# A four-layer network on one core: order of the scan directions, a stream of parts beside the scans, and six product buffers

## The chip, the core and the metric

The kernel runs on one core of a Trainium2 chip, and the metric is the time on the device in microseconds (us). A core has a matrix engine (PE, with its weight loads shown apart as PEld), a vector engine (DVE), a scalar engine for activation functions (ACT), a general engine (POOL) and an engine that issues transfers (SP). Each runs its own queue of instructions in order; they meet at semaphores. The kernel's time before the change is 23055.54 us, the median of three runs that lie between 23043.62 and 23061.29.

## The reference, cut to what matters

Eight images of 56 x 56 tokens with 192 channels go through four layers, each `x = x + layer(group_norm(x))`:

- layer 0 is a gated Toeplitz convolution along h and along w: `p * (o1 + o2) @ o_w`, with `p = silu(x @ p_w)`
- layer 1 is attention in shifted windows of 7 x 7 tokens
- layer 2 is a depthwise 3 x 3 convolution
- layer 3 is a selective scan in four directions:

```
xz = x @ in_proj_w.T; xi, z = split(xz); z = silu(z)
xc = silu(conv3x3(xi))
xs = stack([x_f, x_t, x_f reversed, x_t reversed])
h[t] = exp(delta[t] * A) * h[t-1] + delta[t] * u[t] * B[t]
y[t] = sum over n of h[n, t] * C[n, t] + D * u[t]
y = layer_norm(sum of the four directions) * z;  out = y @ out_proj_w.T
```

Here `x_f` runs through the tokens row by row and `x_t` column by column. There are 384 inner channels (three blocks of 128, index d) and 16 states (eight pairs, index k).

## The kernel before, in words

**Ahead of the scans.** The kernel first computes q * v of layer 0 and the Toeplitz products for all images and writes them to memory. Then it runs the front of image 0 alone. A front is a Python generator that joins five parts: `gate` (the rest of layer 0), `attention`, `conv2`, `inner` (the input projection, the convolution and the activations of layer 3) and `steps`. `steps` computes, in 14 pieces of 448 tokens, the step sizes delta and the coefficients B and C for the two directions of each token order o (o = 0 row by row, o = 1 column by column), and stores them to memory; each piece has one softplus (L870). In `inner` the convolution of a piece of 448 tokens is 9 matmuls into one bank (L802), which ACT then reads (L811). All parts of a front share one buffer, `slab`, so that they follow one another.

**The scans.** Image by image, four directions (slots 0 to 3: slots 0 and 1 row by row, forwards and backwards; slots 2 and 3 column by column), seven chunks of 448 tokens, three d and eight k: 5376 pairs, here also called steps of the loop. One pair g takes these operations:

- POOL: `inject` (L991), hs = du * B for two states
- ACT: two `decay` activations (L1006) into a PSUM bank, and two small copies for the state at the chunk's edge (L996, L1028)
- DVE: the scan itself (L1015)
- `times_c` (L1021), the product hc = h * C, on POOL for k = 1, 4 and 6, on DVE for the other five
- PE: `add_up` (L1036), which adds the two halves of hc into the bank ps_y by a matmul with the identity; the profile has four records for it

There are four hc buffers, so the product of pair g waits until `add_up` of pair g - 4 is done. After eight pairs `sums` adds ps_y into `ysum` (L1046 for slot 0, with the D * x term; L1050 for the other slots; in slots 2 and 3 the target is read and written in steps of a row). du = delta * x (L979, POOL) is made ahead for the next chunk from three loads of x (`load_xc`, L969).

**The parts beside the scans.** While the pairs of image b run, the front of image b + 1 is worked in. A planner, `Parts`, keeps a modelled time for each engine, and after each pair `parts.step` resumes the waiting generators as far as their next piece fits a limit for each engine: for PE up to 5 us after the modelled start of the next scan (n1 + 5.0). The instructions then stand in the engines' queues in the order in which they were emitted. The other kind of part is `finish(b, j)`: the layer norm, gating and output projection for one chunk of 448 tokens (L891 to L934), which reads `ysum`. Since slots 2 and 3 write every row of `ysum`, an image can be finished only after its last slot; its seven finishes therefore run beside slot 0 of the next image, each ahead of the sums that overwrite its tokens. Those of the last image run at the end by themselves.

Before the last chunk of an image's slot 3 ends (d = 1, k = 0 of that chunk, pair 656 of 672) the loads for the next image are issued. At that point a loop with the limit `anything` forces out whatever is left of the front of image b + 1.

Of the kernel before, what the change touches and what calls it, by code (L numbers as in the profile page):

```python
# [15 lines left out]
F32 = mybir.dt.float32  # L16
# [6 lines left out]
H = W = 56  # L23
# [58 lines left out]
def model(ctx: ExitStack, tc: tile.TileContext, a: dict, out: bass.AP):  # L82
# [197 lines left out]
    with (  # L280
# [79 lines left out]


        meter, costs = Meter(tc.nc), {}


        st = wp.tile([CP, 2, NCH, 6], F32, name="gn_st")
# [466 lines left out]
        def steps(b):  # L832

            w_x, xc, rc, dl = carve(slab, 128, (2, ND, 128), (2, ND, CH), (2, CH), (2, ND, CH))
            nc.sync.dma_start(out=w_x, in_=a["w_x"])
            todo = [(o, j) for o in range(2) for j in range(NCH)]

            def load_x(n):
                o, j = todo[n]
                nc.sync.dma_start(out=xc[:, n % 2], in_=xc_d[o][b][:, :, j * CH : (j + 1) * CH])  # L840

            load_x(0)
            yield 0, 0, 8.0
            for n, (o, j) in enumerate(todo):
                tok = slice(j * CH, (j + 1) * CH)
                if n + 1 < len(todo):
                    load_x(n + 1)
                yield 0, 1
                p = bank()
                for d in range(ND):  # L850
                    nc.tensor.matmul(p[:, :CH], w_x[:, o, d, :], xc[:, n % 2, d, :], start=d == 0, stop=d == ND - 1)
                yield 1, 0
                nc.scalar.copy(rc[:, n % 2, :], p[:, :CH])  # L853
                nc.sync.dma_start(out=bc_d[o][b][:, tok], in_=rc[64:, n % 2, :])
                for d in range(ND):
                    yield 0, 2
                    held = []
                    for s in range(2):
                        row = slice(32 * s, 32 * s + R)
                        held.append(bank())  # L860
                        nc.tensor.matmul(  # L861
                            held[s][:, :CH], w_dt[row, o, d * 128 : (d + 1) * 128], rc[row, n % 2, :], start=True, stop=True
                        )
                    yield 2, 0
                    for s in range(2):
                        nc.scalar.activation(
                            dl[:, s, d, :], held[s][:, :CH], AF.Identity, bias=dt_b[:, 2 * o + s, d : d + 1]
                        )
                yield 0, 0
                nc.scalar.activation(dl, dl, AF.Softplus)  # L870
                usual_functions()
                for s in range(2):
                    nc.sync.dma_start(out=dl_d[2 * o + s][b][:, :, tok], in_=dl[:, s])
            yield 0, 0

        def front(b):
# [61 lines left out]
        def scan_view(t, slot, j):  # L938

            if slot < 2:  # L940
                return t[:, j * CH : (j + 1) * CH].rearrange("p (u v) -> p u v", v=H)
            return t.rearrange("p (h w) -> p w h", w=W)[:, 8 * j : 8 * j + 8, :]
# [1 line left out]
        chunks = [  # L944
            (b, slot, j)
            for b in range(B)
            for slot in range(4)
            for j in (range(NCH - 1, -1, -1) if slot % 2 else range(NCH))
        ]
        pairs = [(i, d, k) for i in range(len(chunks)) for d in range(ND) for k in range(NP)]  # L950
# [14 lines left out]

        def load_xc(i, d):
            b, slot, j = chunks[i]
            t = sp.tile([128, CH], F32, name="xcd", bufs=4)
            nc.sync.dma_start(out=t, in_=xc_d[slot // 2][b][:, d, j * CH : (j + 1) * CH])  # L969
            return t  # L970

# [3 lines left out]
            nc.sync.dma_start(out=delta[:, :, 1 : CH + 1], in_=dl_d[slot][b][:, :, j * CH : (j + 1) * CH])  # L975

        def times_x(i, d):
            du = dus[i, d] = sp.tile([128, 1, CH], F32, name="du", bufs=4)
            nc.gpsimd.tensor_mul(du[:, 0, :], deltas[i][:, d, 1 : CH + 1], xcs.pop((i, d)))  # L979

        def tokens(i):
# [35 lines left out]
        def times_c(g):  # L1017
            i, d, k = pairs[g]
            h = hss[g] if on_pool(d, k) else das[g]
            hc = hcs[g] = sp.tile([128, NG, CH], F32, name="hc", bufs=4)  # L1020
            (nc.gpsimd if on_pool(d, k) else nc.vector).tensor_mul(hc, h[:, :, tokens(i)[0]], cms[i, k])  # L1021

        def keep_state(g):
# [15 lines left out]

        def sums(i, d):  # L1040
            b, slot, j = chunks[i]
            y = yps[i, d][:, :CH]
            tok = slice(j * CH, (j + 1) * CH)
            if slot == 0:
                x = xds.pop((i, d))
                nc.vector.scalar_tensor_tensor(ysum[:, d, tok], x, Dsum[:, d : d + 1], y, ALU.mult, ALU.add)  # L1046
                run("D", 0.68)
            else:
                yv = scan_view(ysum[:, d], slot, j)
                nc.vector.tensor_add(yv, yv, y.rearrange("p (u v) -> p u v", v=H))  # L1050
                run("D", 0.87)

        class Parts:

# [7 lines left out]
            def run(self, engine, cost, *after):  # L1062
                self.t[engine] = max(self.t[engine], 0.0, *after) + cost
                return self.t[engine]
# [25 lines left out]
                entry.held, entry.needs, *load = got  # L1090
                entry.ready = at + sum(load)

            def step(self, limit):
                old = [e for e in self.clients if e.held]
                for entry in old + [e for e in self.clients if e not in old]:
                    while entry in self.clients:
                        if entry.held and entry not in old:
                            break
                        if entry.needs + sum(e.held for e in self.clients if e is not entry) > 2:
                            break  # L1100
                        if not self.fits(entry, limit):
                            entry.waits += 1
                            break
                        entry.waits = 0
                        if entry in old:
                            old.remove(entry)
                        self.resume(entry)
# [16 lines left out]
        def drain(work, log=None):  # L1124

            while (next(work, None) if log is None else log_of(work, log)) is not None:
                pass
# [7 lines left out]
        with tc.manual_schedule():  # L1135
            for k in range(NP):
                load_bc(0, k)
            load_delta(0)
            for d in range(ND):
                xcs[0, d] = load_xc(0, d)  # L1140
                times_x(0, d)
            ahead, last = 2, len(pairs) - 1
            parts = Parts()
            run = parts.run
# [6 lines left out]

            def take(g):
                times_c(g)
                after = scanned[g], summed[g - 4] if g > 3 else 0.0
                taken[g] = run("P", 2.0, *after) if on_pool(*pairs[g][1:]) else run("D", 1.09, *after)

            def prepare(g):
# [4 lines left out]
                feed(g)  # L1162
            initial(0), initial(1)
            prepare(0)
            fronts = {}
            ending, anything = None, dict.fromkeys("ADE", 1e9)
            for g, (i, d, k) in enumerate(pairs):
                b, slot, j = chunks[i]
                if i % (4 * NCH) == 0 and d == 0 and k == 0 and b + 1 < B:
                    fronts[b + 1] = parts.add(front(b + 1), "front")  # L1170
                more = i + 1 < len(chunks)
                if more and d == 1 and k == 0:
                    if i + 1 in range(4 * NCH, len(chunks), 4 * NCH):
                        while fronts[b + 1] in parts.clients:
                            parts.step(anything)
                    load_delta(i + 1)
                    for e in range(ND):
                        xcs[i + 1, e] = load_xc(i + 1, e)
                if more and (d, k) in ((1, 6), (1, 7), (2, 0)):
                    times_x(i + 1, d + k - 7 if d == 1 else 2)  # L1180
                    run("P", 1.08)
                pi, pd, pk = pairs[g - 1]
                if g + ahead <= last:
                    feed(g + ahead)
# [14 lines left out]
                if g and pd == ND - 1 and pi + 1 < len(chunks):  # L1199
                    load_bc(pi + 1, pk)  # L1200
                done = (i, d - 1) if d else (i - 1, ND - 1)
                if k == 2 and g > NP and chunks[done[0]][1] == 0:
                    xds[done] = load_xc(*done)
                if slot == 0 and b > 0 and (d, k) == (1, 4):
                    while ending.at < 3:
                        parts.step(anything)
                if k == 4 and g > NP:
                    sums(*done)
                if slot == 0 and b > 0 and ((j, d, k) == (0, 0, 5) or j + 1 < NCH and (d, k) == (2, 4)):
                    while ending in parts.clients:  # L1210
                        parts.step(anything)
                    ending = parts.add(finish(b - 1, j + (d == 2)), "finish")

                n1 = max(parts.t["D"], fed[g + 1], set_[g + 1])
                n2 = n1 + (2.02 if on_pool(*pairs[min(g + 1, last)][1:]) else 3.11)
                parts.step({"A": max(n2, fed[g + 2]) - 0.7, "E": n1 + 5.0, "D": 0.2})
                if g >= 2:
                    add_up(g - 2)
                    summed[g - 2] = run("E", 1.1, taken[g - 2])
# [1 line left out]
                times_c(last)  # L1221
            for g in (last - 1, last):
                add_up(g)
            sums(i, d)
            for j in range(NCH):
                drain(finish(B - 1, j))


def constants():
# [98 lines left out]
```

## Time and profile before

| part of the span | us |
|---|---|
| start to the first scan (Toeplitz, front of image 0) | 3727 |
| image 0, first scan to first scan of image 1 | 2331 |
| images 1 to 6, each | 2453 to 2486 |
| image 7 | 2015 |
| last add-up to the end | 204 |

Busy shares of the span are PE 80%, DVE 72%, POOL 70%, ACT 54%, weight loads 42%. They average over the stages above, and the first stage has hardly any work for POOL. The columns of the views shown later are: for stages, the window, its length, the busy time of PE, PEld, DVE, ACT and POOL with the number of instructions, the share of full clock that PE was granted, the share of the transfer engines and GB/s; for waits, who waited for what, us in total, number of times, and the longest; for a timeline, start, duration, engine, line, operation, shapes and count, and in brackets the idle time ahead of it with what ended it.

### The profile page before, as it was taken

To read this page: it belongs to the slowest core of one execution; us is meant where nothing else is said; L and a number is where in the kernel's file an instruction comes from. 1 tells how busy PE (TensorE), PEld (TensorE's weight loads), DVE (VectorE), ACT (ScalarE), POOL (GpSimd) and SP (SyncE) were. 2 spreads that over 40 slices of the span, in tenths; PEclk is the share of its full clock that TensorE was granted. 3 is DMA by queue.
4 is the path that set the end of the run, shared out by engine and by line. 5 is a ranking of instruction groups with operands and counts; after the bars stand their busy time and mean duration, and the time that the engine had idled before them with its cause. 6 is when DMAs were issued, how large, how long until landed. Compare 5 with 4: busy or idle time off the path is not lost. (4 is left out here: it accounts for less than half of the span.)

```text
span 23083.3 us, 201064 instructions
## 1 busy us (share of the span) xinstructions
PE 18554.5 (80%) x58660; PEld 9730.9 (42%) x58660; DVE 16579.4 (72%) x13156; ACT 12534.0 (54%) x31864; POOL 16157.3 (70%) x8500
## 2 busy tenths in 40 slices
PE   8866678888887878888888888887888798887666
PEld 4566334434443435343543444343434353333323
DVE  3211114997789768986899778976898689877996
ACT  3211225655666565756565566656664657565554
POOL 0000004987789768976898778877897689778997
PEclk9987778999899989998999889998999899988888
DMA  3488225445544455345544454345534553454332
GB/s 89 109 196 178 67 62 171 135 123 168 167 135 131 142 169 146 124 135 172 151 134 129 161 162 137 122 147 177 148 115 146 168 157 119 140 172 139 126 122 89
DMA packets 2536339, 3220.44 MB, mean 140 GB/s; under 512 B 1045261, under 2 KB 2488687, under 8 KB 2504272
## 3 DMA queue, kind: packets, MB, share of 16 engines
q1 hardware_dynamic: 2515010, 3091.32, 45.2%
q0 software_dynamic: 15520, 116.14, 1.3%
q8 instruction: 465, 7.62, 0.1%
q14 instruction: 640, 5.24, 0.1%
q10 hardware_dynamic: 4704, 0.12, 0.0%
HBM read 2631.56 MB, written 575.48 MB: 139 GB/s over the span
## 5 line engine op out<-in xcount | busy, mean ns | idle before, releaser
L991 POOL TENSOR_TENSOR hs<-du,bm 128x896 f32<-128x896 f32 x5376 | 11124.4, 2102 | 110.1 <-DVE ps_a L1015 90.2
L1036 PE MATMUL ps_y<-hc,ident_sb 128*128 128x448 f32 x21504 | 9913.8, 597 | 947.8 <-POOL hc L1021 846.4
L1015 DVE TENSOR_TENSOR_SCAN ps_a<-ps_a,hs 128x898 f32<-128x898 f32 x3360 | 6793.9, 2022 | 1048.5 <-ACT ps_a L1006 871.5
L1006 ACT ACTIVATE ps_a<-delta,A_logs_sb 128x449 f32<-128x449 f32 x10752 | 6859.4, 638 | 322.2 <-DVE hs L1015 35.9
L1036 PEld LDWEIGHTS ps_y<-hc,ident_sb 128*128 128x128 f32 x21504 | 4339.0, 210 | 5095.4 <-issue 3594.3
L1021 POOL TENSOR_TENSOR hc<-hs,cm 128x896 f32<-128x896 f32 x2016 | 4067.0, 2017 | 2757.2 <-DVE hs L1015 1574.0
L1015 DVE TENSOR_TENSOR_SCAN hs<-ps_a,hs 128x898 f32<-128x898 f32 x2016 | 4064.5, 2016 | 810.3 <-ACT ps_a L1006 779.3
L1021 DVE TENSOR_TENSOR hc<-ps_a,cm 128x896 f32<-128x896 f32 x3360 | 3668.9, 1092 | 1166.1 <-PE ps_y L1036 883.2
L1028 ACT COPY state<-ps_a 128x2 f32<-128x2 f32 x3359 | 528.6, 157 | 4109.0 <-DVE hc L1021 4106.4
L979 POOL TENSOR_TENSOR du<-delta,xcd 128x448 f32<-128x448 f32 x672 | 716.0, 1066 | 1266.1 <-DMA xcd<-xc 1266.1
L263 PE MATMUL ps_tz<-tzx,tm 112*112 112x112 f32 x4608 | 889.3, 369 | 463.5 <-issue 294.7
L802 PE MATMUL ps_f<-slab 128*128 128x448 f32 x2646 | 1096.9, 551 | 85.0 <-DMA slab<-dg_d 58.0
L277 POOL DMA_DIRECT2D o<-tzx x192 | 97.8, 513 | 1490.9 <-DVE tzx L269 1340.1
L263 PEld LDWEIGHTS ps_tz<-tzx,tm 112*112 112x112 f32 x4608 | 883.8, 199 | 469.2 <-issue 468.1
L269 DVE COPY tzx<-ps_tz 112x448 f32<-112x448 f32 x288 | 179.9, 625 | 1172.3 <-PE ps_tz L263 862.0
L996 ACT COPY hs<-state 128x2 f32<-128x2 f32 x4608 | 817.5, 177 | 2.7 <-POOL hc L1021 2.6
L76 PE MATMUL ps_f<-slab 96*96 96x448 f32 (+6 forms) x2306 | 745.3, 519 | 76.1 <-DMA slab<-x 37.4
L269 ACT COPY tzx<-ps_tz 112x448 f32<-112x448 f32 x288 | 153.2, 532 | 1198.1 <-PE ps_tz L263 1067.2
L632 PE MATMUL ps_f<-ident_sb,slab 98*98 98x98 f32 x1344 | 337.9, 322 | 576.3 <-ACT slab L625 576.3
L734 PE MATMUL ps_f<-slab 96*96 96x448 f32 x1764 | 728.9, 549 | 46.4 <-DVE slab L721 46.4
L802 PEld LDWEIGHTS ps_f<-slab 128*128 128x128 f32 x2646 | 509.4, 193 | 598.0 <-issue 528.7
L861 PE MATMUL ps_f<-slab,w_dt_sb 12*128 12x448 f32 x1176 | 507.5, 787 | 309.8 <-ACT slab L853 234.9
(215 smaller groups left out, 17788.8 us busy)
## 6 DMA issues: line engine op xcount, KB each, us to landing
bm<-bc SPq DMA_DIRECT2D x1792, 448.0 KB
cm<-bc SPq DMA_DIRECT2D x1792, 448.0 KB
xcd<-xc SPq DMA_DIRECT2D x840, 224.0 KB
dl<-slab SPq DMA_DIRECT2D x224, 672.0 KB
delta<-dl SPq DMA_DIRECT2D x224, 672.0 KB
tzx<-qv SPq DMA_DIRECT2D x192, 588.0 KB
o<-tzx POOLq DMA_DIRECT2D x192, 588.0 KB, 16.3
slab<-x SPq DMA_DIRECT2D x224, 336.0 KB
```

The source lines that it names most:

```text
L76: return f(*args, **kw)
L263: nc.tensor.matmul(po[:, c, :], t[:, c2 + c, :], x[:, :, c1 + c2 + c], start=True, stop=True)
L734: nc.tensor.matmul(p[:CP, :CH], dg[:, k, t, :], xp[:, u, k, dy : dy + 8, dx : dx + W], start=t == 0, stop=t == 8,)
L802: nc.tensor.matmul(p[:, :CH], dg[:, t, :], xp[:, 8 * j + dy : 8 * j + dy + 8, dx : dx + W], start=t == 0, stop=t == 8,)
L979: nc.gpsimd.tensor_mul(du[:, 0, :], deltas[i][:, d, 1 : CH + 1], xcs.pop((i, d)))
L991: nc.gpsimd.tensor_mul(hs[:, :, tokens(i)[0]], dus[i, d].to_broadcast([128, NG, CH]), bms[i, k])
L996: nc.scalar.copy(hss[g][:, :, tokens(i)[1]], src)
L1006: nc.scalar.activation(dA[:, n, :], deltas[i][:, d, at : at + CH + 1], AF.Exp, scale=negA[:, slot, d, c : c + 1])
L1015: nc.vector.tensor_tensor_scan(h, dA, hs, 0.0, ALU.mult, ALU.add)
L1021: (nc.gpsimd if on_pool(d, k) else nc.vector).tensor_mul(hc, h[:, :, tokens(i)[0]], cms[i, k])
L1028: nc.scalar.copy(states[i][:, d, NG * k : NG * k + NG], h[:, :, tokens(i)[2]])
L1036: nc.tensor.matmul(yps[i, d][:, :CH], ident, hcs[g][:, n, :], start=k + n == 0, stop=k + n == NP + NG - 2)
```

## The change

Five things are altered together.

- The directions of an image go 2, 3, 0, 1: column by column first, row by row last, and the last one backwards. When a chunk of slot 1 is done, its tokens have all four directions, so its finish can start beside the following pairs of the same image. Only the last chunk's finish falls beside the next image, or for image 7 at the end. `steps` computes o = 1 first to match.
- The fronts form one stream. The front of the next image is added as soon as the one ahead is through, whichever image is being scanned. Instead of forcing out the whole front at the end of an image, the loop asks for each chunk whether its step sizes are there (`made`), and if not forces that front alone (`only`) up to that piece.
- There are six hc buffers in place of four.
- To make room for them, x and du have two buffers each in place of four, and are made one d at a time: the load at k = 0, the product at k = 3, for the d after the current one.
- The planner's limit for PE is n1 + 8.0 in place of n1 + 5.0.

The diff, cut to its core:

```diff
-            todo = [(o, j) for o in range(2) for j in range(NCH)]
+            todo = [(o, j) for o in (1, 0) for j in range(NCH)]
...
+                made.add((b, o, j))
...
-            for slot in range(4)
+            for slot in (2, 3, 0, 1)
...
-            t = sp.tile([128, CH], F32, name="xcd", bufs=4)
+            t = sp.tile([128, CH], F32, name="xcd", bufs=2)
...
-            du = dus[i, d] = sp.tile([128, 1, CH], F32, name="du", bufs=4)
+            du = dus[i, d] = sp.tile([128, 1, CH], F32, name="du", bufs=2)
...
-            hc = hcs[g] = sp.tile([128, NG, CH], F32, name="hc", bufs=4)
+            hc = hcs[g] = sp.tile([128, NG, CH], F32, name="hc", bufs=6)
...
-            if slot == 0:
-                x = xds.pop((i, d))
-                nc.vector.scalar_tensor_tensor(ysum[:, d, tok], x, Dsum[:, d : d + 1], y, ALU.mult, ALU.add)
+            if slot == 2:
+                x = xds.pop((i, d)).rearrange("p (u v) -> p u v", v=H)
+                nc.vector.scalar_tensor_tensor(yv, x, Dsum[:, d : d + 1], y, ALU.mult, ALU.add)
...
-                after = scanned[g], summed[g - 4] if g > 3 else 0.0
+                after = scanned[g], summed[g - 6] if g > 5 else 0.0
...
-                if i % (4 * NCH) == 0 and d == 0 and k == 0 and b + 1 < B:
-                    fronts[b + 1] = parts.add(front(b + 1), "front")
+                if ahead_of not in parts.clients and b_next < B:
+                    ahead_of = parts.add(front(b_next), "front")
+                    b_next += 1
...
-                    if i + 1 in range(4 * NCH, len(chunks), 4 * NCH):
-                        while fronts[b + 1] in parts.clients:
-                            parts.step(anything)
+                    b1, slot1, j1 = chunks[i + 1]
+                    while (b1, slot1 // 2, j1) not in made:
+                        parts.step(anything, ahead_of)
                     load_delta(i + 1)
-                    for e in range(ND):
-                        xcs[i + 1, e] = load_xc(i + 1, e)
-                if more and (d, k) in ((1, 6), (1, 7), (2, 0)):
-                    times_x(i + 1, d + k - 7 if d == 1 else 2)
-                    run("P", 1.08)
+                if k in (0, 3) and (d + 1 < ND or more):
+                    at = (i, d + 1) if d + 1 < ND else (i + 1, 0)
+                    if k == 0:
+                        xcs[at] = load_xc(*at)
+                    else:
+                        times_x(*at)
+                        run("P", 1.08)
...
-                if slot == 0 and b > 0 and ((j, d, k) == (0, 0, 5) or j + 1 < NCH and (d, k) == (2, 4)):
+                pb, pslot, pj = chunks[i - 1]
+                if i and pslot == 1 and (d, k) == (0, 5):
                     while ending in parts.clients:
-                        parts.step(anything)
-                    ending = parts.add(finish(b - 1, j + (d == 2)), "finish")
+                        parts.step(anything, ending)
+                    ending = parts.add(finish(pb, pj), "finish")
...
-                parts.step({"A": max(n2, fed[g + 2]) - 0.7, "E": n1 + 5.0, "D": 0.2})
+                parts.step({"A": max(n2, fed[g + 2]) - 0.7, "E": n1 + 8.0, "D": 0.2})
...
+            while parts.clients:
+                parts.step(anything)
             sums(i, d)
-            for j in range(NCH):
-                drain(finish(B - 1, j))
+            drain(finish(b, j))
```

More of the change, by code (lines that the diff above doesn't have):

```diff
@@ L362, in model @@
         meter, costs = Meter(tc.nc), {}
+        made = set()
         st = wp.tile([CP, 2, NCH, 6], F32, name="gn_st")
@@ L1041, in sums @@
             b, slot, j = chunks[i]
-            y = yps[i, d][:, :CH]
-            tok = slice(j * CH, (j + 1) * CH)
-            if slot == 0:
-                x = xds.pop((i, d))
-                nc.vector.scalar_tensor_tensor(ysum[:, d, tok], x, Dsum[:, d : d + 1], y, ALU.mult, ALU.add)
-                run("D", 0.68)
-            else:
-                yv = scan_view(ysum[:, d], slot, j)
-                nc.vector.tensor_add(yv, yv, y.rearrange("p (u v) -> p u v", v=H))
-                run("D", 0.87)
+            y = yps[i, d][:, :CH].rearrange("p (u v) -> p u v", v=H)
+            yv = scan_view(ysum[:, d], slot, j)
+            if slot == 2:
+                x = xds.pop((i, d)).rearrange("p (u v) -> p u v", v=H)
+                nc.vector.scalar_tensor_tensor(yv, x, Dsum[:, d : d + 1], y, ALU.mult, ALU.add)
+            else:
+                nc.vector.tensor_add(yv, yv, y)
+            run("D", 0.87)
         class Parts:
@@ L1091, in resume, with step @@
                 entry.ready = at + sum(load)
-            def step(self, limit):
+            def step(self, limit, only=None):
                 old = [e for e in self.clients if e.held]
                 for entry in old + [e for e in self.clients if e not in old]:
+                    if only is not None and entry is not only and not entry.held:
+                        continue
                     while entry in self.clients:
@@ L1138, in model @@
             load_delta(0)
-            for d in range(ND):
-                xcs[0, d] = load_xc(0, d)
-                times_x(0, d)
+            xcs[0, 0] = load_xc(0, 0)
+            times_x(0, 0)
             ahead, last = 2, len(pairs) - 1
@@ L1164, in model @@
             prepare(0)
-            fronts = {}
+            ahead_of, b_next = None, 1
             ending, anything = None, dict.fromkeys("ADE", 1e9)
@@ L1201, in model @@
                 done = (i, d - 1) if d else (i - 1, ND - 1)
-                if k == 2 and g > NP and chunks[done[0]][1] == 0:
+                if k == 2 and g > NP and chunks[done[0]][1] == 2:
                     xds[done] = load_xc(*done)
-                if slot == 0 and b > 0 and (d, k) == (1, 4):
+                if i % (4 * NCH) == 0 and b > 0 and (d, k) == (1, 4):
                     while ending.at < 3:
-                        parts.step(anything)
+                        parts.step(anything, ending)
                 if k == 4 and g > NP:
                     sums(*done)
-                if slot == 0 and b > 0 and ((j, d, k) == (0, 0, 5) or j + 1 < NCH and (d, k) == (2, 4)):
+                pb, pslot, pj = chunks[i - 1]
+                if i and pslot == 1 and (d, k) == (0, 5):
                     while ending in parts.clients:
-                        parts.step(anything)
-                    ending = parts.add(finish(b - 1, j + (d == 2)), "finish")
+                        parts.step(anything, ending)
+                    ending = parts.add(finish(pb, pj), "finish")
                 n1 = max(parts.t["D"], fed[g + 1], set_[g + 1])
                 n2 = n1 + (2.02 if on_pool(*pairs[min(g + 1, last)][1:]) else 3.11)
-                parts.step({"A": max(n2, fed[g + 2]) - 0.7, "E": n1 + 5.0, "D": 0.2})
+                parts.step({"A": max(n2, fed[g + 2]) - 0.7, "E": n1 + 8.0, "D": 0.2})
                 if g >= 2:
```

## The prediction

> **What bounds the kernel now.** I read the span by stages first. The first row is image 3 as a whole, whose pairs run while the front of image 4 is worked in beside them; the second is image 7, which has no front beside it; then the stages of image 3: gate with finish, attention, conv2, inner, steps, and the stall at the end.
>
> ```profile
> core 0: us, PE busy (x) PEld busy (x) DVE busy (x) ACT busy (x) POOL busy (x), PEclk, DMA share, GB/s
> 11014.00:13481.00 2467.00, 2060.65 (x6412) 1029.43 (x6411) 2013.10 (x1546) 1505.95 (x3865) 2003.73 (x1037) 0.90 0.47 145
> 20861.00:22873.00 2012.00, 1375.34 (x2978) 644.74 (x2976) 1843.91 (x1197) 1064.51 (x2767) 1988.19 (x1032) 0.86 0.39 126
> 11014.00:11561.00 547.00, 485.92 (x1858) 281.40 (x1856) 442.44 (x345) 305.77 (x700) 448.02 (x238) 0.95 0.56 153
> 11561.00:12386.00 825.00, 673.16 (x2385) 334.30 (x2385) 768.01 (x651) 578.65 (x1814) 759.78 (x391) 0.91 0.40 123
> 12394.00:12621.00 227.00, 192.57 (x478) 85.72 (x479) 205.75 (x164) 91.17 (x243) 168.38 (x87) 0.93 0.46 139
> 12635.00:13153.00 518.00, 440.87 (x1119) 219.03 (x1119) 377.66 (x242) 287.61 (x649) 399.25 (x205) 0.91 0.47 153
> 13153.00:13361.00 208.00, 167.94 (x396) 69.63 (x396) 159.20 (x101) 164.65 (x324) 170.80 (x87) 0.84 0.58 201
> 13361.00:13440.00 79.00, 62.58 (x96) 22.32 (x96) 3.31 (x3) 47.91 (x58) 1.39 (x1) 0.59 0.39 133
> ```
>
> Image 7 runs its 672 pairs in 2012 us with POOL busy for 1988: there POOL is the bound, 3.0 us a pair (2.89 where no finish runs: 486 us for 168). Images 1 to 6 take about 2467 us each by the start times of the scans. No engine is full over such an image: DVE is busy for 2013 us, POOL for 2004. Some 450 us of an image DVE idles, and the question is what ends that. DVE's longest waits in image 3:
>
> ```profile
> DVE hc L1021 <- PE ps_y L1036: 132.4, 85, 9.2
> DVE hs L1015 <- ACT ps_a L1006: 113.4, 16, 75.1
> DVE ps_a L1015 <- ACT ps_a L1006: 78.4, 42, 8.2
> ```
>
> One wait of 75 us is the stall of the sixth stage: DVE 3 us busy, POOL 1. The timeline has ACT and PE alone there, with one softplus after another at 15.7 us a chunk: the front of image 4 was not finished, and the loop before the last chunk of slot 3 forces the rest out. The gaps between scans at pair 656 of images 0 to 6 are 59.5, 84.2 and five times 78, together 535 us. The other waits for ACT come to 117 us. The 132 us are the product buffer hc (four of them), held until PE has added it up. They lie mostly in the inner stage, and the timeline shows why:
>
> ```profile
> 12906.32 1.67 PE L1036 MATMUL ps_y<-hc,ident_sb 128*128 128x448 f32 x4
> ...
> 12907.82 2.42 PE L802 MATMUL ps_f<-slab 128*128 128x448 f32 x6
> ...
> 12908.02 1.09 DVE L1021 TENSOR_TENSOR hc<-ps_a,cm 128x896 f32<-128x896 f32 x1 [2.57 <-PE ps_y L1036]
> ...
> 12910.28 0.64 ACT L811 ACTIVATE slab<-ps_f,cb_sb 128x448 f32<-128x448 f32 x1 [5.20 <-PE ps_f L802]
> ```
>
> Starts are 0.375 us apart without a gap: 6 convolution records and 4 of add-up per pair are 3.75 us, and the pairs come at 3.75 us. In the 63 pairs beside the 21 convolution banks PE is full; only outside them can a buffer help. The tail is the last item: the add-ups end at 22879 and seven finishes follow with nothing beside them, 204 us or 29 each.
>
> ```profile
> 22873.03 6.28 PE ps_y L1036 x16
> 22879.31 2.27 PE ps_f L891 x6
> 22881.61 1.56 DVE slab_f L898
> ```
>
> **What the Trainium skill says.** "Perfetto Trace Analysis", section Identifying the Most-Contended Engine, judges PE by its weight loads and not by matmul time. In inner these are 42% busy while PE has nothing to spare over long stretches; each load takes 0.19 of a 0.375 us spacing here, so about half is full. The spacing decides. "TensorE: Matmul & The Clock Gate", section What's actually happening: an idle PE falls back to half clock and activity lifts it. The trace agrees: clock 0.59 in the stall, 0.91 in inner. "PSUM — Partial Sum Buffer", section Engine vs sequencer instructions: ACT, DVE and POOL queues are strict FIFO. The trace agrees: ACT sits 5.20 us before L811, and the decays behind it go out only afterwards. "ScalarE: Activation LUTs", section What ACT_TABLE_LOAD costs, has 1.28 us for a table load, which the trace has too; the drain it adds does not appear as a gap.
>
> **The change, part by part.**
>
> *Finish beside slot 1.* Six of the seven closing finishes go under the last image's pairs: 6 x 29 = 175 us off the end; one stays. In exchange image 0, which had none, gets a group of seven finishes beside its pairs. Such a group costs 640 - 551 = 90 us beside a gate (slot 0 of image 4 against image 0's) and 553 - 486 = 67 us beside no front (image 7's slots). The new neighbours, the inner and steps stages, are unseen: a group's own DVE work in image 3, 20 us, is the floor, its PE, ACT and POOL work all exposed (126 + 46 + 55) the ceiling. I keep 90. Sum: **-85**.
>
> *One stream of fronts.* At the old pace a front needs 656 pairs and then some 5 chunks at 58/9 = 6.4 pairs (nine softplus in the fifth stage), about 688 pairs in an image of 672. Before, the shortfall of every image was forced at its end. Now only the first chunk of o = 1 must exist there, the next one 24 pairs later, and the remaining 13 chunks (84 pairs) have time. The drift of 16 pairs an image uses that up only by image 6. Gain 535; the 35 chunks that lay in the stalls (counted by L870) now run beside pairs, at 3.59 - 2.89 = 0.70 us more a pair x 6.4 = 4.5 us each, -158 of the gain; about 77 us go for the quick pairs after a stall (15 in 41.6 us, 12 us fewer than usual) and another 25 for a forced rest in the last images. **-275**.
>
> *Six product buffers.* Of the 132 us, PE's full stretch accounts for 63 x (3.75 - 2.82) = 58, 2.82 being DVE's own pair (2.02 + 5/8 x 1.09 + 1/8 of a sum of 0.97). That stays. The other 74, jitter, x 7 = 520; two buffers more give PE about 6 us of further lag, as against waits of 9.2 at most; I take two thirds, **-340** (bounds 0 and -520). At each full stretch DVE also runs two pairs further ahead once: 2 us x about 4 stretches x 7, **-60**.
>
> *PE limit n1 + 8.* This removes no PE work. It lets the planner pack convolution banks into fewer pairs, perhaps 2.3 instead of 3, so that fewer pairs share PE's full time, and those come later at 2.89: up to 30 us an image; I take **+60** in all (0 to 210). ACT behind L811 waits longer, which costs nothing where PE is full.
>
> *One x tile at a time.* xcd and du fall from four to two buffers; the load is issued at k = 0 and used at k = 3, three pairs (9 us or more) later, where before it had six. A late load holds POOL, behind which inject, and so DVE, wait. Nearest row: the ysum operation L1046 uses its xcd two pairs after the load, and waited 7 us in 147 uses. The issue queue is in order, and loads behind a finish's transfer, which waits for PE, can be later. 0 to 250, **+30**.
>
> *o = 1 first in the steps part.* Its x is stored last, so the first load waits for a 1568 KB store; PE already waits 117 us in 7 fronts there. 0 to 90, **+20**. The strided ysum operation moves from slot 2's add to the multiply-add, while slot 0's becomes a contiguous add: 0.97 + 0.66 before, about 1.02 + 0.60 after; nothing.
>
> Sum: -85 - 275 - 340 - 60 + 60 + 30 + 20 = -650; 23055 - 650 = **22405 us**.
>
> **Rivals.** (1) More: all jitter waits go and the fronts keep ahead of the images: -85 - 350 - 520 - 60 = -1015, so 22040. For it: DVE's 2013 us of work leave room. Against: PE at 85 to 89% busy in the stages concerned. (2) Less: PE is the bound wherever DVE waits for it, and buffers only move the wait. Then the tail and the stalls alone: -85 - 275 + 60 + 30 + 20 = -250, 22805. For it: 77 of 132 us lie in inner. (3) Slower: the deeper PE queue holds ACT at each result (L811, L456, L866, L789, L786: 1447 us in all fronts), growing by 8/5, +870, all passed on to the scans: -360 + 870, 23565. Against it: those waits lie largely where PE is full.
>
> **How the numbers follow.** Forecast 0.55, more 0.20, less 0.19, slower 0.06. The range 21950 to 22820 takes in both middle rivals and leaves out the slower case and the far end of (1). Faster by over 0.2%: all but the slower case and a little of (2), 0.93; same 0.02; slower 0.05.
>
> **What would show it.** Right: no gap of 60 us between scans at pair 656; image 7 longer than 2012 us, images 1 to 6 near 2380; DVE's waits for ps_y at a third outside inner, about 60 us an image left; one finish after the last add-up. Wrong: DVE waiting for PE at ysum, POOL waiting for xcd in du, or ACT's waits for ps_f up by more than half. If the front falls behind by more than 84 pairs, forced stretches come back at each chunk of slot 2.

## The result and the profile after

The changed kernel takes 22528.0 us (22518.07 to 22537.83), the kernel before 23049.58 us beside it: ratio 0.9776, 95% interval 0.9759 to 0.9793, so 2.2% faster. The forecast was 22405 us, 650 us off; 522 us came off. The mechanism of the forecast is only half right, as the experiments show: two of its terms were far too small and one far too large, and by luck they nearly cancel.

Where the time went, by the starts of the scans: images 1 to 6 take 2386 to 2428 us each in place of 2453 to 2486, image 0 takes 2362 in place of 2331, image 7 is the same (2016 against 2012), and the part after the last add-up shrinks from 204 to 32 us. The windows of the changed kernel shown here are image 3 as a whole, the gate alone, inner with its finishes, steps up to the end of image 3, and the next 79 us, in which the last four chunks of steps run beside the first pairs of image 4.

```profile
10914.00:13311.00 2397.00, 2040.15 (x6413) 1020.07 (x6412) 2014.33 (x1546) 1497.49 (x3867) 2006.59 (x1037) 0.92 0.49 150
...
11009.00:11425.00 416.00, 389.51 (x1504) 217.47 (x1502) 380.33 (x290) 246.31 (x562) 364.13 (x189) 0.98 0.60 168
...
12503.00:13064.00 561.00, 484.71 (x1273) 249.46 (x1272) 395.95 (x261) 314.44 (x717) 432.59 (x225) 0.92 0.49 159
13080.00:13311.00 231.00, 208.69 (x519) 90.69 (x516) 163.75 (x108) 185.87 (x361) 190.03 (x99) 0.84 0.60 202
13311.00:13390.00 79.00, 59.97 (x162) 27.33 (x160) 51.55 (x35) 62.32 (x116) 54.73 (x29) 0.87 0.52 176
```

The stall is gone: in the last 79 us DVE is busy for 52 us, in the stall of before it was 3. No two scans of the changed kernel start more than 16 us apart, where before there was one gap of 60 to 84 us in each of seven images. The gate, now without finishes, takes 416 us for 124 pairs, 3.4 us a pair (3.8 before with them); inner, with finishes, takes 561 for 140, 4.0 a pair (3.8 before without). DVE and POOL do the same work per image as before, 2014 and 2007 us.

DVE's longest waits in image 3, to set beside those of before:

```profile
DVE ps_a L1017 <- ACT ps_a L1008: 145.2, 72, 5.3
DVE hs L1017 <- ACT ps_a L1008: 53.4, 27, 6.5
```

The 132 us of waits for the product buffers are gone; the forecast had left about 60 of them in place. But the waits for ACT, 192 us before of which 75 were the stall, are 199 us without any stall. Something has filled the place. Over all images, before:

```profile
DVE hc L1021 <- PE ps_y L1036: 883.2, 594, 9.2
DVE ps_a L1015 <- ACT ps_a L1006: 871.5, 295, 344.4
DVE hs L1015 <- ACT ps_a L1006: 779.3, 106, 81.0
```

and after:

```profile
DVE ps_a L1017 <- ACT ps_a L1008: 1365.3, 500, 349.9
DVE hs L1017 <- ACT ps_a L1008: 337.5, 188, 8.0
```

The products waited 883 us for PE before and 48 us after. The scans waited 1651 us for the decays before, 513 of them in the stalls, and 1703 after without a stall. Some 350 us of each sum are the wait for the first scan of all, which every version has. The tail has one finish:

```profile
22496.10 7.97 PE ps_y L1038 x16
22504.08 2.27 PE ps_f L893 x6
...
22532.31 0.62 DVE slab_f L935
```

### The profile page after: what moved, and what is told of

Its sections match the earlier page's. It is cut to its first block, busy times and chain, and to the rows that moved or that the text cites. A ratio compares the mean times of both kernels' runs of the same rounds, so it can differ in the third digit from the quotient of the medians.

```text
span 22536.1 us, 200417 instructions
## 1 busy us (share of the span) xinstructions
PE 18327.5 (81%) x58660; PEld 9644.0 (43%) x58660; DVE 16594.4 (74%) x13156; ACT 12468.3 (55%) x31864; POOL 16169.7 (72%) x8500
## 5 line engine op out<-in xcount | busy, mean ns | idle before, releaser
L1017 DVE TENSOR_TENSOR_SCAN hs<-ps_a,hs 128x898 f32<-128x898 f32 x2016 | 4065.2, 2016 | 481.1 <-ACT ps_a L1008 337.5
L618 ACT ACTIVATE slab<-slab,mxs 98x98 f32<-98x98 f32 x1344 | 489.4, 365 | 359.7 <-DVE mxs L615 359.7
```

Of the source, the lines that this page charges most:

```text
L1017: nc.vector.tensor_tensor_scan(h, dA, hs, 0.0, ALU.mult, ALU.add)
```

## The experiments

All times are set against the kernel before on the same chip, whose median moves between 23049 and 23106 us from chip to chip, so the ratios are compared and not the times. First the theories, formed from the waits above. **A**: the two extra buffers let PE lag further; ACT, which stands in order behind PE's results, passes the lag on to the decays and so to the scans, and the buffers give nothing. **B**: the buffers gave what was forecast, and something else lost it. Later came **C**: PE's own work fills the stretches concerned, so that it does not matter which wait DVE sits in; and **D**: not the buffers but the order that the planner makes of them does the harm.

**Four hc buffers again** (`e1_hc4`):

```diff
-            hc = hcs[g] = sp.tile([128, NG, CH], F32, name="hc", bufs=6)
+            hc = hcs[g] = sp.tile([128, NG, CH], F32, name="hc", bufs=4)
-                after = scanned[g], summed[g - 6] if g > 5 else 0.0
+                after = scanned[g], summed[g - 4] if g > 3 else 0.0
```

> The changed kernel with four hc buffers again (pool and planner), the rest of the change as it is. Theory A (the waits for hc were only handed on: with six buffers PE lags further, and ACT, which stands in order behind its results, passes the lag to the scans): about the time of the changed kernel, 22450 to 22650 us; DVE's waits for ps_y at the products come back to 800 us or more, and its waits for decay fall from 1874 us by 500 or more. Theory B (the buffers gave what was forecast, and something else lost it): 22800 to 22950 us.

Measured: 22594.05 us, ratio 0.9787 (0.9774 to 0.9800). The waits for hc are back (927 us), and the scans' waits for ACT, those for its small copies included, are down from 1874 to 1298 us. Theory A as to both waits and time.

**The limit back at 5** (`e2_lim5`), with six buffers:

```diff
-                parts.step({"A": max(n2, fed[g + 2]) - 0.7, "E": n1 + 8.0, "D": 0.2})
+                parts.step({"A": max(n2, fed[g + 2]) - 0.7, "E": n1 + 5.0, "D": 0.2})
```

> The changed kernel with the planner's PE limit back at n1 + 5.0, six hc buffers kept. Theory A: the deeper PE queue feeds ACT's waits for PE; with the shorter one DVE's waits for decay fall by 300 us or more and the kernel is the same or faster than the changed one, 22250 to 22530 us. Theory B: the limit packs the parts better and pays for itself, so without it 22600 to 22800 us.

Measured: 22513.89 us, ratio 0.9750 (0.9737 to 0.9764). The time is theory A's, but not the wait: the scans wait 1898 us for ACT, no less than with the limit at 8. Some of it is new: gaps of 34 to 35 us have come up at pair 656 of images 4 to 6, where the fronts fall behind. Even without these, about 100 us in all, the waits would not have fallen by the 300 us of theory A. So the limit does not feed most of those waits; by the first run, the buffers do.

**Both undone** (`e3_hc4_lim5`), the two edits above together:

> The changed kernel with four hc buffers and n1 + 5.0: order of directions, finishes, stream and the late x loads alone. Theory A: 22450 to 22600 us, near the changed kernel, so that buffers and limit together give nothing. Theory B: 22850 to 22950 us, the buffers' 340 us missing.

Measured: 22440.34 us, ratio 0.9719 (0.9706 to 0.9733). Faster than the changed kernel by 0.6%, and just below theory A's own range: buffers and limit together do not give nothing, they cost. B is out. The order of directions, the finishes, the stream and the late x loads alone give 648 us (0.0281 of 23055).

**Four x buffers** (`e4_hc4_x4`), beside the first run; the instructions are in the same order on every engine:

```diff
-            t = sp.tile([128, CH], F32, name="xcd", bufs=2)
+            t = sp.tile([128, CH], F32, name="xcd", bufs=4)
-            du = dus[i, d] = sp.tile([128, 1, CH], F32, name="du", bufs=2)
+            du = dus[i, d] = sp.tile([128, 1, CH], F32, name="du", bufs=4)
```

> As the run with four hc buffers and n1 + 8.0, and with four buffers for x and du in place of two (loads and products at the same places). If the two x buffers hold loads back, this is 20 to 100 us faster than that run; if the loads are late only because they are issued three pairs ahead, it is the same within 20 us.

Measured: 22600.19 us, ratio 0.9789 (0.9776 to 0.9803): the same. Two buffers are enough; POOL waits 91 us for xcd with two and 86 with four.

**The planner's PE costs as measured** (`e5_calib` on the changed kernel, `e6_calib_hc4_lim5` on the run with both undone):

```diff
-    TIMES = {"tensor": ("E", 0.04, 1.25e-3), "scalar": ("A", 0.2, 0.83e-3),
+    TIMES = {"tensor": ("E", 0.0, 1.68e-3), "scalar": ("A", 0.2, 0.83e-3),
...
-                    summed[g - 2] = run("E", 1.1, taken[g - 2])
+                    summed[g - 2] = run("E", 1.5, taken[g - 2])
```

> The changed kernel with the planner's PE costs as the trace has them: 0.75 us for a 448-column matmul in place of 0.60, 1.5 us for an add-up in place of 1.1. If ACT waits because the planner sends the readers of PE's results too early (theory A), DVE's waits for decay fall from 1874 us to under 1300 and the time to 22000 to 22350 us. If the waits come from PE work that fills the stretch in any order (theory C), the waits only spread over more pairs and the time stays at 22450 to 22650 us; if the fronts then fall behind, forced stretches come back and it is slower still.

> The same measured PE costs with four hc buffers and n1 + 5.0, beside the run with those two undone alone (0.972 of the kernel before). Theory A: waits for hc (832 us there) and for decay (1207) both fall, 21950 to 22300 us. Theory C: the same as that run within 0.3%.

Measured: 22859.25 us, ratio 0.9907 (0.9893 to 0.9920), and 22784.41 us, 0.9873 (0.9860 to 0.9887). Both are slower by more than 1%, for the last reason named in the first expectation: a planner that knows what PE costs gives the fronts less of it, they fall behind, and forced stretches come back at pairs 655 and 656 of images 1 to 6, 182 to 201 us an image in the first run and about 165 in the second. DVE's waits in the first show them as its longest:

```profile
DVE ps_a L1017 <- ACT ps_a L1008: 1012.1, 365, 352.9
DVE hs L1017 <- ACT ps_a L1008: 904.9, 211, 129.4
```

The 129.4 us is a forced stretch. (The 352.9 us in the other line is the wait for the first scan of all.) The scans' waits for ACT, 2113 us in the first run and 1828 in the second, hold up to 1100 and 1000 us of such stretches, so the rest may well have fallen, as theory A has it; the forced stretches more than take it back. Theories A and C are not told apart by these two runs.

**Directions and finishes without the stream** (`e7_no_stream`, four buffers, limit 5):

```diff
-                if ahead_of not in parts.clients and b_next < B:
+                if i == (b_next - 1) * 4 * NCH and d == 0 and k == 0 and b_next < B:
...
-                    while (b1, slot1 // 2, j1) not in made:
+                    while b1 > b and ahead_of in parts.clients:
```

> Directions 2, 3, 0, 1 with the finishes beside slot 1, four hc buffers and n1 + 5.0, but each front is begun with its image and forced out whole at pair 656, as before. Forecast's split (finish 85, stream 275 us): 0.996 of the kernel before. If the stream has its gain from the stalls alone, gaps of 60 us or more come back at pair 656, larger than before since finish and steps now share a stretch: 60 to 130 us each, and the time is 0.993 to 1.002 of the kernel before.

**The stream without the rest** (`e8_stream_only`), the kernel before with the stream's lines alone: `made`, `only`, a new front as soon as the last one is through, and each chunk asking for its own step sizes.

> The kernel before with the stream of fronts alone: the directions stay 0, 1, 2, 3, finishes beside slot 0, four hc buffers, n1 + 5.0, x loads as before; each chunk asks for its own step sizes. Forecast's step: 275 us less than before, 0.988. If the stalls (535 us) were pure loss, 0.977 to 0.980; if the drift of 16 pairs an image brings forced stretches back, 0.992 or more.

Measured: 22785.44 us, ratio 0.9873 (0.9859 to 0.9886), for the finishes, with gaps of 79 to 81 us back at pair 656 of each image; and 22660.85 us, 0.9822 (0.9809 to 0.9835), for the stream. So the finishes give 293 us alone and 237 on top of the stream (0.9822 to 0.9719), the stream 410 us alone and 355 on top of the finishes (0.9873 to 0.9719). The figures for the finishes hold the late x loads and the order of `steps` as well, which no run undoes by themselves. Both were forecast too low, 85 and 275. Neither expectation held its number: the stream lies between the forecast and pure loss, and the finishes are better than any case named.

**Six buffers in the order of four** (`e10_six_plan4`): limit 5, six hc buffers, and a planner that believes in four. Against the run with both undone only the `bufs` of hc differ, and each engine has the same instructions in the same order.

> Six hc buffers, n1 + 5.0, but the planner still believes in four (summed[g - 4]): every engine has the instructions of the run with four buffers and n1 + 5.0 (0.9719 of the kernel before) in the same order, only the buffers differ. Theory A (the physical lag does harm, since ACT stands in order behind its results): 0.9735 to 0.976, like the run with six buffers and n1 + 5.0 (0.975); DVE's waits for decay near 1900 us. Theory D (the order that the planner emits did the harm, buffers alone give something): 0.965 to 0.970, waits for decay near 1200 us and for hc under 200. Theory C (PE's work fills those stretches whatever DVE waits for): 0.971 to 0.973, the waits for hc moved to decay or to other waits one for one.

Measured: 22484.97 us, ratio 0.9738 (0.9725 to 0.9751), against 0.9719 (0.9706 to 0.9733). D is out: two buffers more, nothing else altered, and nothing is gained. The time lies just inside theory A's range and just above theory C's, and the scans' waits for ACT are near theory A's figure, so the number alone would speak for A. DVE's longest waits with four buffers,

```profile
DVE ps_a L1017 <- ACT ps_a L1008: 912.9, 312, 350.0
DVE hc L1023 <- PE ps_y L1038: 832.0, 540, 13.5
DVE hs L1017 <- ACT ps_a L1008: 174.8, 65, 5.8
```

and with six:

```profile
DVE ps_a L1017 <- ACT ps_a L1008: 1354.8, 489, 350.2
DVE hs L1017 <- ACT ps_a L1008: 386.2, 213, 11.9
DVE ps_a L1017 <- POOL hs L993: 142.6, 141, 6.4
```

The products' 832 us are all gone. The scans' waits for the decays rise from 1088 to 1741, by 653 us, and DVE's remaining waits for PE from 218 to 419, by 201: 854 us in place of 832. That the two sums agree is no finding of its own, since the same work in nearly the same time leaves nearly the same idle time; what it shows is where the waits went. The timelines of one convolution bank in both show how one of them passes over. With four buffers:

```profile
12525.58 0.63 ACT L812 ACTIVATE slab<-ps_f,cb_sb 128x448 f32<-128x448 f32 x1 [3.27 <-PE ps_f L803]
...
12527.08 1.09 DVE L1023 TENSOR_TENSOR hc<-ps_a,cm 128x896 f32<-128x896 f32 x1 [2.57 <-PE ps_y L1038]
...
12536.86 0.63 ACT L812 ACTIVATE slab<-ps_f,cb_sb 128x448 f32<-128x448 f32 x1 [3.27 <-PE ps_f L803]
```

With six:

```profile
12557.05 0.63 ACT L812 ACTIVATE slab<-ps_f,cb_sb 128x448 f32<-128x448 f32 x1 [4.48 <-PE ps_f L803]
...
12557.67 1.31 ACT L1008 ACTIVATE ps_a<-delta,A_logs_sb 128x449 f32<-128x449 f32 x2
...
12559.08 2.04 DVE L1017 TENSOR_TENSOR_SCAN ps_a<-ps_a,hs 128x898 f32<-128x898 f32 x1 [3.10 <-POOL hs L993]
...
12561.20 1.09 DVE L1023 TENSOR_TENSOR hc<-ps_a,cm 128x896 f32<-128x896 f32 x1
...
12568.33 0.64 ACT L812 ACTIVATE slab<-ps_f,cb_sb 128x448 f32<-128x448 f32 x1 [4.38 <-PE ps_f L803]
```

With six buffers the product no longer waits. In its place ACT waits 1.1 to 1.2 us longer at its bank, the decays behind the bank end at 12558.98, and the scan that needs them starts 0.1 us later, after a wait of 3.10 us. The view puts that wait down to POOL, but the `inject` of this scan had ended at 12546.50. But look at the spacing of ACT's reads: 12525.58 to 12536.86 and 12557.05 to 12568.33, 11.28 us in both, and seven banks in a row take 67.7 and 67.6 us. That is PE's work: 18 convolution records and 3 x 4 of add-up at 0.375 us are 11.25. Theory C holds there: PE is full, and a buffer only chooses whose wait its backlog shows up in. Of the 832 us, 505 lie in the 21 stretches of the inner convolutions, which last 1828 us with four buffers and 1814 with six. In both runs these stretches hold 4517 PE records of 448 columns at 0.375 us and 426 of 224 columns at 0.19 us, together 1775 us, 97 to 98% of their length. The other 327 us lie where PE is not full over longer times, and they gave nothing either: block for block of 56 pairs the two runs differ by 8 us at most. That ACT's order passes the wait on is shown there by the sums alone, and what sets the pace in those stages was not separated. The run is slower by 0.2%, and the two intervals overlap. In the profiled executions the loss lies in the gate: each of its seven stages is 4 to 11 us longer with six buffers, 52 us in all, and the scans' waits for ACT there rise from 130 to 223 us, though the products had waited only 16. So some of theory A's harm may be real in the gate; why, and whether it would hold over more executions, stays open. In the convolutions only its handing on is shown.

**The product du two pairs later** (`e9_x_at_k5`), so that the load of x has five pairs in place of three; four buffers and limit 5:

```diff
-                if k in (0, 3) and (d + 1 < ND or more):
+                if k in (0, 5) and (d + 1 < ND or more):
```

> Four hc buffers, n1 + 5.0, and du made at k = 5 in place of k = 3, with the load of x still at k = 0: five pairs ahead in place of three. If POOL's waits for xcd (160 us in the run with k = 3) reach the end, 0.967 to 0.970 of the kernel before; if POOL has slack there, 0.971 to 0.973 and those waits fall under 40 us all the same.

Measured: 22556.28 us, ratio 0.9767 (0.9754 to 0.9780). POOL's waits for xcd fall from 160 to 3 us, and the kernel is slower by 0.5% all the same, outside both ranges of the expectation. The waits did not reach the end. The moved product shifts the planner's time for POOL, and with it the order of the instructions on every engine. The fronts fall behind: gaps of 28 to 39 us come up at pair 656 of images 4 to 6, and the products' waits rise from 832 to 969 us. But images 0 to 3, without such gaps, are longer too, by 77 us together, so why the run is slower was not settled.

**The limit at 3** (`e11_hc4_lim3`), four buffers; the edit is that of the limit with 3.0.

> Four hc buffers and the planner's PE limit at n1 + 3.0, beside n1 + 8.0 (0.9787 of the kernel before) and n1 + 5.0 (0.9719). If a shorter modelled PE queue spreads the parts over more pairs and so fills PE less densely (the reading of 8.0 against 5.0), 0.964 to 0.970 as long as the fronts keep up; if they fall behind, gaps of 20 us and more at pair 656 and 0.972 to 0.982.

Measured: 22398.21 us, ratio 0.9694 (0.9680 to 0.9707), the fastest of all by its median, 0.8% below the changed kernel; its interval just meets that of the run with both undone. The first case of the expectation, with the gaps of the second: 69 to 71 us at pair 656 of images 3 to 6, so the fronts fall behind and the time is still better. Conv2, which took 59 pairs at 3.8 us with the limit at 5 or 8, takes 66 at 3.5. The products wait less than in any run so far with four buffers; the 68.1 us is a forced stretch.

```profile
DVE hc L1023 <- PE ps_y L1038: 488.6, 347, 8.7
DVE hs L1017 <- ACT ps_a L1008: 472.9, 82, 68.1
```

**Readers of PE's results placed 2 us later** (`e12_margin`), four buffers and limit 5:

```diff
                 entry.held, entry.needs, *load = got
-                entry.ready = at + sum(load)
+                entry.ready = at + on_pe + sum(load)
```

with `on_pe` 2.0 after a piece whose last operation is PE's, else 0.

> Four hc buffers and n1 + 5.0, and the planner takes each result of PE to be ready 2 us later than it models, so that its readers are placed later in ACT's and DVE's queues; PE's modelled time itself is unchanged. If readers placed too early cost time (ACT's 1484 us of waits for PE holding decays), those waits fall to 1000 us or less, DVE's waits for decay (1207) by 200 or more, and the time is 0.962 to 0.970 of the kernel before; if PE's own work sets the stretches, 0.970 to 0.975, the waits moved to the products; if the longer chains slow the fronts, forced stretches at pair 656 and 0.975 to 0.985.

Measured: 24104.45 us, ratio 1.0432 (1.0418 to 1.0447), slower than the kernel before and far outside all three ranges of the expectation. The chain of a front is what breaks: gate takes 186 pairs in place of 125, attention 329 in place of 257, and most of inner is forced out at pairs 655 and 656, some 466 us in each of images 1 to 6. DVE then waits in order for the front's weights:

```profile
DVE slab L397 <- DMA slab<-in_w_in_dram: 1562.1, 20, 119.4
DVE hs L1017 <- ACT ps_a L1008: 1124.5, 81, 138.9
```

While it lasts the gate's pairs do come at 3.1 us. This suggests that early readers are the price for fronts that keep up with the images; whether a planner could have both was not tried.

## Why the prediction was right, and where its steps were not

The time lies within the stated range and the direction held. The range had to be wide to take in two rivals, and the sum came near by luck. Step by step:

- **Finish beside slot 1, -85.** The tail is right (172 us off, forecast 175). The cost of the exchange was mis-sized and had the wrong sign: a group of finishes was put at 90 us, the same beside inner and steps as beside a gate. With the stream in place, image 0 pays 52 us for its new group (2286 to 2338), but images 1 to 6 become 18 us shorter each (2399 to 2381 on average) and image 7 by 21. The term measures -237 on top of the stream, the x loads and the order of `steps` included. A gate without finishes drops to 3.3 us a pair and from about 130 pairs to 125, and inner and steps, which take the finishes, give back less than that. Why a finish is cheaper there was not separated further.
- **One stream of fronts, -275.** The mechanism is right, the size too small: -355 on top of the finishes, -410 alone. Of the 535 us of stalls little comes back: the steps stage of the stream-only run goes at 3.6 to 4.0 us a pair, and the only forced stretch is one gap of 47 us in image 6. (A slip in the sum changes nothing here: 12 us in each of seven images are 84 us, not 77.)
- **Six product buffers, -340 and -60.** This is the step that failed. The waits for hc went, and further than forecast: 48 us were left in all, where about 60 an image had been expected to stay in PE's full stretches. The gain did not come: with the limit at 5, six buffers cost 71 us (0.9719 to 0.9750), or 44 with the order of instructions held fixed; with the limit at 8 they give 25 (0.9787 to 0.9776). The last two are within the noise. The forecast was -400. Its first half was sound: in the kernel before, the 21 stretches of the inner convolutions last 1651 us for 2646 convolution records and 421 pairs, and at 0.375 us a record PE has (2646 + 4 x 421) x 0.375 = 1624 us of work in them, 98%; 479 of the 883 us of waits lie there, 68 an image where the forecast set 58 aside. What failed is "The other 74, jitter, x 7 = 520; ... I take two thirds": outside those stretches the time did not come back with the wait either. The waits passed to the decays and to DVE's other waits for PE. The 60 us for running ahead did not come, presumably because DVE, held at ACT, cannot run ahead; this was not tested by itself. The sentence of the prediction that ACT's longer wait behind L811 "costs nothing where PE is full" is what the runs bear out inside the convolution stretches. The second rival had the better reason on this point. As for the Trainium skill, "PSUM — Partial Sum Buffer", section Engine vs sequencer instructions, has the ACT and DVE queues as strict FIFO. The timelines agree: with six buffers ACT waits 4.48 us at its bank, and the decays behind it start only then, at 12557.67, and release the scan. By that order the wait passes from the product to the decays.
- **PE limit n1 + 8, +60.** Right in sign, and with six buffers in size: +60 us (0.9750 to 0.9776), +157 with four (0.9719 to 0.9787). The packing is there: 415 pairs beside the inner convolutions with 8.0, 452 with 5.0, which is less than the 2.3 for 3 that was assumed.
- **One x tile at a time, +30.** POOL's waits for xcd come to 114 us between the first and the last scan, and DVE's at the first add into `ysum` to 35. More buffers change nothing, and a longer lead of the load takes POOL's waits away and gains nothing. The term was not undone by itself; nothing suggests that it cost much.
- **o = 1 first, +20.** PE's wait for the first load of steps fell, from 117 to 79 us in seven fronts. The two ysum operations cost 1.03 and 0.60 us as expected. This term was not undone by itself either.

So the finishes and the stream, forecast at -360, or -310 with the x loads and the order of `steps`, measured -648; the buffers and the limit, forecast at -340 - 60 + 60, measured about +127 together. The sum was near by this cancelling, not by the sizes.

## What to carry to other kernels

When an engine waits for a buffer that a nearly full engine has to empty, more buffers may only move the wait: set that engine's work against the stretch's length before counting the wait as a gain, and ask which wait comes next in the same engines' order. To tell buffers from order in a planned kernel, change the buffer count and keep the planner's belief, so that the instructions stay the same. And where a loop stops at a boundary to force out work that is late, ask for each piece only when it is needed: here the stalls had been 535 us, and the stream gave 355 to 410.

## What the runs showed that had not been expected

Small edits to the planner move the time by as much as the resources they are about. The edit that took away 157 us of POOL's waits made the kernel 0.5% slower. Giving the planner the measured PE costs made it 1.3 to 1.5% slower: with costs set too low the fronts had kept level with the images, and with the measured ones they fell behind. In the inner convolutions PE's spacing of 0.375 us a record held to a part in a hundred over seven banks, 67.7 and 67.6 us, whatever the other engines waited for.
